# Query, key and value projections as seven products of quarters, four steps a set, in a transformer block on one core

## The chip, the core and the metric

The kernel runs on one core of a Trainium2 chip. The metric is the device time of one execution, in microseconds (us). The engines are TensorE (PE in the profile, its weight loads PEld), VectorE (DVE), ScalarE (ACT), GpSimd (POOL) and SyncE (SP), which issues the DMAs. Each works through its own instructions in the order in which the program emits them; waits between engines are semaphores.

## The reference

Two layers over 4 sequences of 1024 rows of 512 fp32 values, all in fp32. The first is a graph attention over 20 neighbours; the second, where the change lies, is a transformer block with modulation from a condition vector `c`:

```python
def _attention(x, W_qkv, W_out, b_out):          # 16 heads of 64, INNER = 1024
    qkv = x @ W_qkv                               # 512 -> 3 * 1024
    q, k, v = jnp.split(qkv, 3, axis=-1)
    ...
    attn = jnp.einsum('bqhd,bkhd->bhqk', q, k) * scale
    attn = jax.nn.softmax(attn, axis=-1)
    out = jnp.einsum('bhqk,bkhd->bqhd', attn, v).reshape(Bq, Tq, INNER)
    return out @ W_out + b_out

def _ff(x, W1, b1, W2, b2):                       # 512 -> 2048 -> 512
    return jax.nn.gelu(x @ W1 + b1, approximate=False) @ W2 + b2
```

Around both stand a normalization of the rows, a modulation (scale and shift from `c`), a gate and a residual sum.

## The kernel before

**Three stages.** The graph attention (32 tiles of 128 rows) ends at 457 us. Then comes the attention, a loop of 256 slots, to about 2346 us. The MLP fills the rest; it multiplies in seven products of quarters (the function `seven`: a 2 x 2 block product with 7 products in place of 8, with sums of the blocks made beforehand by `sums_a` and `sums_b`).

**A slot** (loop over `s`) handles 128 query rows of one pair of heads: for each of the 4 batches, 8 pairs `gp`, 8 row tiles `t`. It emits: the first transpose on DVE of the weights of the slot before (`turn`, L1000); the scores of both heads on TensorE (`scores`, L965) into two PSUM tiles of two banks, tag `sc`; the row maxima on DVE (`largest`, L976); the exponentials on ACT, with row sums (`weights`, L982); a reciprocal on DVE and the scaling of head 0 on ACT (`scaled`, L987, L989); the second transpose of the slot before; a reciprocal and the scaling of head 1 on POOL (L991). Four DMAs per head and pair of slots (L1004, SP) put the transposed weights in place. The score tiles have two buffers in all, so the scores of a slot wait for the exponentials of the slot before.

**Fill.** At the end of a slot stands other work, taken from a list `fill`. An entry has a window of slots, a size in units and a place within the slot (0 loads, 1 `attend`, 2 projections, 3 transposes of normalized rows, 4 sums and row work). A planner spreads the units evenly over the slots; in one slot the entries go by place and then by their position in the list. The entries that matter here:

- `mm_qk` (L409): half of one accumulation for the query or key of one pair of heads, 128 outputs x 512 rows, 1 unit; 8 for each of the 32 sets. ACT evacuates it: query L418, key L421 with its elements reordered.
- `mm_v` (L910): the values of four heads, 128 rows x 256 columns, 1 unit; 8 for each of the 16 sets; evacuated in pairs by ACT (L918).
- `attend` (L927): weights times values for 256 query rows of a pair of heads, 2 units; evacuated by ACT (L936).
- `project` (L945): output projection of 128 rows, 1 unit; DVE adds it to the residual rows (L953) and, in the last group, takes the statistics for the next normalization (L111).
- `norm_load`, `norm_row` (DVE, L356), `norm_T` (PE transposes L374, ACT L379 into `hT`, two tiles of 512 rows a batch).
- `load_qk`, `load_v`, `load_out`, `load_rows` (SP) and `gate_out`, `gate_rows` (POOL, L881, L891).

All these products write to one rotating set of four PSUM banks: `MM = dict(tag="mm", bufs=4)`. A tile in a rotating set waits until the reader of the tile that had the bank before is done.

**The end of the loop.** From slot 244 the first MLP unit begins: weights are loaded (`load_w1`), POOL makes their sums (`mlp_weights`) and the sums of the rows (`mlp_rows`), and seven steps of `seven` stand in slots 249 to 255, one a slot.

Of the kernel before, what the change touches and what calls it, by code (L numbers as in the profile page):

```python
# [19 lines left out]
P = 128  # L20
# [21 lines left out]
def cond_block_kernel(  # L42
# [49 lines left out]
    sel = cst.tile([P, B, P], F32, name="sel")  # L92
    for k in range(4):
        q = slice(32 * k, 32 * k + B)
        nc.vector.tensor_copy(sel[q], ident[q, q].unsqueeze(2).to_broadcast([B, B, P]))
# [23 lines left out]
    def spread(k, b, pg):  # L119

        q = slice(32 * k, 32 * k + B)
        nc.tensor.matmul(pg, lhsT=sel[q, b, :], rhs=gates[q, :], start=True, stop=True)
        return pg
# [6 lines left out]
    with ExitStack() as gctx:  # L130
# [16 lines left out]
        with ExitStack() as sctx:  # L147
# [58 lines left out]
            for b in range(B):  # L206
                pr = sps.tile([P, F], F32, name="pr", tag="s")
                nc.tensor.matmul(pr, lhsT=sel[:B, b, :], rhs=qrows, start=True, stop=True)
                evac(b, qrB[:, b, :], pr)
# [173 lines left out]
        def load_w(held, key, tag, src, cols):  # L383

            t = rp.tile([P, FC, 2, P], F32, name=tag, tag=tag, bufs=2)
            for k, col in enumerate(cols):
                nc.sync.dma_start(t[:, :, k, :], src[:, col : col + P].rearrange("(c p) f -> p c f", p=P))
            held[key] = t
# [58 lines left out]
        def seven(get, opens, short, lhs, rhs, nk, room, done):  # L447
# [5 lines left out]
            a, b, c, d, s5 = ({} for _ in range(5))  # L453

            def product(t, which, fresh):
                for q in range(2):
                    for k in range(nk):
                        nc.tensor.matmul(  # L458
                            t[:, q * HB : (q + 1) * HB],
                            lhsT=lhs(which, q, k),  # L460
                            rhs=rhs(which, k),
# [5 lines left out]
            def bank_of(held, name):  # L467
                held[0] = get(name)
                if opens and name in ("mb", "md"):
                    nc.tensor.matmul(held[0], lhsT=ident, rhs=hT[1, 0][:, 0, :], start=True, stop=True)  # L470
                return held[0]

            def step0():
                product(bank_of(a, "ma"), 0, True)
                nc.scalar.copy(bank_of(b, "mb"), a[0])  # L475

            def step1():
                product(bank_of(c, "mc"), 4, True)
                s5[0] = short()
                nc.scalar.copy(s5[0], c[0])  # L480

            def step2():
                product(b[0], 5, False)
                nc.vector.tensor_tensor(bank_of(d, "md"), b[0], s5[0], ALU.add)

            def step3():
                product(a[0], 1, False)
                done(0, 0, a[0])

            def step4():  # L490
                product(b[0], 6, False)
                s6 = room()
                nc.vector.tensor_tensor(s6, b[0], s5[0], ALU.add)
                done(1, 1, s6)

            def step5():
                product(d[0], 2, False)
                done(0, 1, d[0])

            def step6():  # L500
                product(b[0], 3, False)
                done(1, 0, b[0])

            return step0, step1, step2, step3, step4, step5, step6

        ex, hs, hx, tx = {}, {}, {}, {}

        def mlp_rows():  # L510

            h = hT[1, 0]
            if not tx:
                tx[0] = rp.tile([P, FC, VB * P], F32, name="tx", tag="hT", bufs=2)
            o = [tx[0][:, k, :].rearrange("p (c r) -> p c r", c=2) for k in range(3)]
            sums_b(nc.gpsimd, o, h[:, :2, :HB], h[:, :2, HB:], h[:, 2:, :HB], h[:, 2:, HB:])

        def mlp_weights(e, i, home):

            ex[i] = home()  # L520
            o = [ex[i][:, k * HB : (k + 1) * HB].rearrange("p (c f) -> p c f", c=2) for k in range(3)]
            w = w1g[i]
            sums_a(e, o, w[:, :2, 0, :], w[:, 2:, 0, :], w[:, :2, 1, :], w[:, 2:, 1, :])

        def up_lhs(p):
            def lhs(which, q, c):
                i = 2 * p + q
                at = {4: 0, 5: 1, 2: 2}.get(which)
                if at is not None:
                    return ex[i][:, at * HB + c * P : at * HB + (c + 1) * P]  # L530
                h, f = {0: (0, 0), 1: (0, 1), 3: (1, 1), 6: (1, 0)}[which]
                return w1g[i][:, 2 * f + c, h, :]

            return lhs

        def up_rhs(which, c):
            at = {4: 0, 5: 1, 3: 2}.get(which)
            if at is not None:
                return tx[0][:, at, c * HB : (c + 1) * HB]
# [253 lines left out]
        for s in range(-4, NTA + 2):  # L793
# [44 lines left out]
            if s == 25:  # L838
# [3 lines left out]
                load_v(0, 1)  # L842
# [5 lines left out]

    vp = ctx.enter_context(tc.tile_pool(name="vp", bufs=1, side="right", reuse_waits="tile"))
# [4 lines left out]
    with ExitStack() as actx:  # L854
        ap_ = actx.enter_context(tc.tile_pool(name="ap", bufs=1, reuse_waits="tile"))
        MM = dict(tag="mm", bufs=4)
# [14 lines left out]
        def load_out(b, g):  # L871

            t = op_.tile([P, 2, F], F32, name="wout", tag="wout", bufs=2)
# [28 lines left out]
        def mm_v(b, g, n):  # L902

            if (b, g) not in vt:
                vt[b, g] = vp.tile([P, NT, GW], F32, name="v", tag="v", bufs=2)
            if n % 2 == 0:
                part["v", n // 2] = ps.tile([P, 2, GW], F32, name="pvv", **MM)
            pt = part["v", n // 2]
            for c in range(FC):
                nc.tensor.matmul(  # L910
                    pt[:, n % 2, :],
                    lhsT=hT[0, 2 * b + n // VB][:, c, n % VB * P : (n % VB + 1) * P],
                    rhs=wv[b, g][:, c].rearrange("p k f -> p (k f)"),
                    start=(c == 0),
                    stop=(c == FC - 1),
                )
            if n % 2 == 1:
                nc.scalar.copy(vt[b, g][:, n - 1 : n + 1, :], pt)  # L918

        def attend(b, gp, k):  # L920
# [13 lines left out]
            if p == 0 and k == 0:  # L934
                oT[b, g] = op_.tile([P, 2, S], F32, name="oT", tag="oT", bufs=2)
            nc.scalar.copy(  # L936
                oT[b, g][:, p, k * QB : (k + 1) * QB].rearrange("p (t u q) -> p u t q", t=QT, u=4),
# [3 lines left out]
        def project(b, g, n):  # L941

            po = ps.tile([P, F], F32, name="pout", **MM)
            for p in range(2):
                nc.tensor.matmul(  # L945
                    po,
                    lhsT=oT[b, g][:, p, n * P : (n + 1) * P],
# [78 lines left out]

        def add(lo, hi, units, place, f, *args):
            fill.append((lo, hi, units, place, lambda: f(*args)))

        for b in range(B):  # L1030
            s0 = b * NP * NT
            for gp in range(NP):
                g, p = divmod(gp, 2)
                at = s0 + gp * NT
                if gp == 0 and b > 0:
                    for h, (ld, rws, tr) in enumerate(
                        ((-18, (-15, -14, -13, -12), -11), (-10, (-9, -9, -8, -8), -7))
# [6 lines left out]

                if at > 0:
                    for k in range(2):
                        for n in range(2):
                            for half in range(2):

                                lo = at - (8 if gp > 0 else (9, 5)[n])  # L1050
                                add(lo, at - (2 if gp < NP - 1 else 4), 1, 2, mm_qk, b, gp, k, n, half, bank)
                if p == 0:
                    for n in range(NT):
                        lo, hi = (at - 12, at + 1) if g > 0 else (max(at - (9, 5)[n // VB], 0), at + 3)
                        add(lo, hi, 1, 2, mm_v, b, g, n)
# [4 lines left out]
                if p == 1:  # L1060
                    for n in range(NT):
                        lo = at + QT * (NB - 1) + LAG + (3 if g == 0 else 2)
                        add(lo, lo + (7 if g == NGRP - 1 else 10), 1, 2, project, b, g, n)
                if gp == 0:
                    lo = max(at - 3, 0)
                    add(lo, lo, 0.5, 2, gates_of, b)
                    for n in range(NT):

                        lo = at + (1 + n if b == 0 else 13 + n // 2)
                        add(lo, lo, 0, 0, load_rows, b, n)  # L1070
                        add(lo + 1, lo + 1, 0, 4, gate_rows, b, n)
                if p == 0:
                    add(at + 8, at + 8, 0, 0, load_out, b, g)
                    add(at + 9, at + 9, 0, 4, gate_out, b, g)
                if at - 16 >= 0:
                    add(at - 16, at - 16, 0, 0, load_qk, b, gp)
                if p == 0 and at - 24 >= 0:
                    add(at - 24, at - 24, 0, 0, load_v, b, g)
# [3 lines left out]
        add(NS - 18, NS - 18, 0, 0, norm_load, 1, 0)  # L1082
# [4 lines left out]
        for i, at in enumerate((NS - 14, NS - 11, NS - 13, NS - 12)):  # L1087
            add(at, at, 0, 0, load_w1, i, "wqk" if i < 2 else "wv")
        add(NS - 7, NS - 7, 0, 4, mlp_rows)
        for i in range(2):  # L1090
            add(NS - 9 + i, NS - 9 + i, 0, 4, mlp_weights, nc.gpsimd, i, home_q(("qT", "kT")[i]))

        def short():
            return op_.tile([P, F], F32, name="s", tag="s", bufs=2)
# [10 lines left out]
        first = seven(bank, True, short, up_lhs(0), up_rhs, 2, room0, done0)  # L1105
        for k, f in enumerate(first):
            at = NS - 7 + k
            add(at, at, (1.5, 1, 1.5, 1, 1, 1, 1)[k], 2, f)
# [3 lines left out]
        used = {}  # L1112
        for w, f in zip(where, fill):
# [239 lines left out]
```

## Time and profile before

| | |
|---|---|
| median of 3 runs | 3178.59 us (3177.89 to 3180.68) |
| profiled execution | 3184.05 us, its span 3182.3 us |
| attention loop, first score product to that of slot 255 | 457.15 to 2346.02 us |
| mean clock granted to TensorE | 0.993 of full |
| key and query projections (L409), TensorE busy | 475.1 us, 1024 rows |
| value projections (L910) | 238.3 us, 1024 rows |
| scores (L965), attend (L927), output projection (L945) | 517.1, 472.1, 243.2 us |
| maxima (L976) and transposes (L1000) on DVE | 601.3, 633.9 us |
| exponentials (L982) and scaling (L989) on ACT | 570.7, 291.1 us |
| scaling on POOL (L991) | 730.5 us |

How to read the profile: a group line names line, engine, operation, output and inputs, shapes and count, then the busy time, the mean time of one instruction, and the engine's idle time just before them with what ended it. Matmul rows overlap each other, so their mean (604 ns for L409) is longer than the distance between two starts, and the busy time of a group is that of the union. A timeline line begins with start and length in us from the span's start. An idle time in square brackets names what the engine waited for.

### The profile page before, as it was taken

What the parts mean: (1) busy time and instruction counts of PE and PEld (TensorE: products, weight loads), DVE (VectorE), ACT (ScalarE), POOL (GpSimd) and SP (SyncE); (2) the same over time, 40 slices, a digit from 0 to 9 for tenths busy, and PEclk for the clock granted to TensorE, in tenths of its full rate; (3) what the DMA queues carried; (4) which work ended last, traced back from release to release, by engine and by line L of the source; (5) the groups of instructions that cost most, each with busy time, mean ns of one, the idle gap of its engine ahead of it and who ended that gap; (6) DMA issues with size and microseconds to landing.
All of it is one profiled execution on the core that took longest, in us unless ns stands there. A gap on an engine that the chain in (4) does not pass through costs nothing.

```text
span 3182.3 us, 39273 instructions
## 1 busy us (share of the span) xinstructions
PE 3142.3 (99%) x14571; PEld 1938.9 (61%) x14571; DVE 1941.9 (61%) x2718; ACT 1406.2 (44%) x2312; POOL 1066.0 (33%) x580
## 2 busy tenths in 40 slices
PE   8999999999999999999999999999999999999999
PEld 5666665544444544454544454544457888888888
DVE  2688866777767777767777767777864332223222
ACT  1344446555555555555555555555641221112211
POOL 1344325344343544343544343544432101111020
PEclk8999999999999999999999999999999999999999
DMA  4233317776777776777776777776862101101010
GB/s 164 71 102 98 119 45 184 160 177 153 175 170 180 177 177 154 175 170 180 178 177 154 176 171 179 178 176 147 193 162 88 40 27 40 40 14 40 27 40 14
DMA packets 272850, 405.29 MB, mean 127 GB/s; under 512 B 24660, under 2 KB 97424, under 8 KB 272660
## 3 DMA queue, kind: packets, MB, share of 16 engines
q1 hardware_dynamic: 272660, 402.78, 50.6%
q8 instruction: 116, 1.90, 0.2%
q14 instruction: 74, 0.61, 0.1%
HBM read 109.08 MB, written 25.17 MB: 42 GB/s over the span
## 4 chain that ended last, share of the span: by engine, by line
PE 86%; DVE 5%; SPq 2%; DMA 2%; issue 2%; POOL 2%; ACT 1%; POOLq 0%; DVEq 0%; ACTq 0%
PE psc L965 14%; PE pqk L409 14%; PE pav L927 12%; PE pvv L910 7%; PE pout L945 6%; PE mbd L458 5%; PE mbu L458 5%; PE mad L458 3%; PE mau L458 3%; PE pa L647 2%; PE pf L607 2%; PE mcd L458 2%; PE mdd L458 2%; SPq L1004 2%; PE mdu L458 2%
## 5 line engine op out<-in xcount | busy, mean ns | idle before, releaser
L991 POOL TENSOR_SCALAR w<-w,sm 128x1024 f32<-128x1024 f32 x256 | 730.5, 2853 | 1074.3 <-DVE sm L987 1074.3
L982 ACT ACTIVATE w<-psc,mx 128x1024 f32<-128x1024 f32 x512 | 570.7, 1115 | 769.3 <-DVE mx L976 768.8
L976 DVE TENSOR_REDUCE mx<-psc 128x1 f32<-128x1024 f32 x512 | 601.3, 1215 | 261.9 <-PE psc L965 260.0
L1000 DVE STREAM_TRANSPOSE wd<-w 128x1024 f32<-128x1024 f32 x512 | 633.9, 1238 | 143.4 <-ACT w L989 118.0
L965 PE MATMUL psc<-kT,qT 64*128 64x512 f32 x2048 | 517.1, 616 | 2.0 <-DVE xs L723 0.9
L409 PE MATMUL pqk<-hT,wqk 128*128 128x512 f32 x1024 | 475.1, 604 | 0.0
L927 PE MATMUL pav<-wT,v 128*64 128x256 f32 x4096 | 472.1, 382 | 1.1 <-DMA wT<-wd 0.8
L927 PEld LDWEIGHTS pav<-wT,v 128*64 128x64 f32 x4096 | 284.4, 137 | 226.8 <-issue 78.9
L965 PEld LDWEIGHTS psc<-kT,qT 64*128 64x128 f32 x2048 | 185.8, 186 | 273.7 <-issue 161.1
L409 PEld LDWEIGHTS pqk<-hT,wqk 128*128 128x128 f32 x1024 | 185.0, 189 | 246.8 <-issue 244.2
L989 ACT ACTIVATE w<-w,sm 128x1024 f32<-128x1024 f32 x256 | 291.1, 1137 | 0.0
L945 PE MATMUL pout<-wout,oT 128*128 128x512 f32 x512 | 243.2, 610 | 0.0
L910 PE MATMUL pvv<-wv,hT 128*128 128x256 f32 x1024 | 238.3, 384 | 0.0
L910 PEld LDWEIGHTS pvv<-wv,hT 128*128 128x128 f32 x1024 | 190.8, 190 | 66.3 <-issue 43.8
L442 POOL TENSOR_TENSOR tx<-hT 128x512 f32<-128x512 f32 x8 | 10.2, 1269 | 565.0 <-DVE hT L381 565.0
L945 PEld LDWEIGHTS pout<-wout,oT 128*128 128x128 f32 x512 | 90.0, 189 | 134.5 <-issue 118.2
L647 PE MATMUL pa<-kp,sfT 128*128 128x320 f32 x512 | 143.5, 433 | 1.4 <-ACT sfT L622 1.4
L475 ACT COPY mbu<-mau 128x512 f32<-128x512 f32 x30 | 17.1, 570 | 287.8 <-PE mau L458 287.8
L647 PEld LDWEIGHTS pa<-kp,sfT 128*128 128x128 f32 x512 | 94.8, 190 | 38.2 <-ACT sfT L622 1.9
L953 DVE TENSOR_TENSOR xr<-pout,xr 128x512 f32<-128x512 f32 x128 | 85.2, 676 | 51.6 <-PE pout L945 51.1
L607 PE MATMUL pf<-wx,xT 128*128 128x512 f32 x256 | 115.3, 593 | 0.3 <-DVE pf L589 0.3
L458 PE MATMUL mad<-w,hs 128*128 128x256 f32 x512 | 113.1, 379 | 0.0
(276 smaller groups left out, 3559.3 us busy)
## 6 DMA issues: line engine op xcount, KB each, us to landing
wT<-wd SPq DMA_DIRECT2D x1024, 256.0 KB
wqk<-in_w_qkv SPq DMA_DIRECT2D x64, 256.0 KB
xs<-in_x SPq DMA_DIRECT2D x36, 256.0 KB
x1d<-xs SPq DMA_DIRECT2D x32, 256.0 KB
xl<-x1d SPq DMA_DIRECT2D x32, 256.0 KB
wv<-in_w_qkv SPq DMA_DIRECT2D x32, 256.0 KB
xr<-x1d SPq DMA_DIRECT2D x32, 256.0 KB
wout<-in_w_out SPq DMA_DIRECT2D x16, 512.0 KB
```

The costliest lines, as they stand in the source:

```text
L409: nc.tensor.matmul(pt, lhsT=wqk[b, gp][:, c, k, :], rhs=hT[0, 2 * b + n][:, c, :], start=(c == 0), stop=(c == FC - 1),)
L458: nc.tensor.matmul(t[:, q * HB : (q + 1) * HB], lhsT=lhs(which, q, k), rhs=rhs(which, k), start=(fresh and q == 0 and k == 0), stop=(k == ...
L647: nc.tensor.matmul(pas[i][:, n, :HF], lhsT=sfT2[i][:, c, :], rhs=kp[:, b, c, n * HF : (n + 1) * HF], start=False, stop=(c == FC - 1), skip ...
L910: nc.tensor.matmul(pt[:, n % 2, :], lhsT=hT[0, 2 * b + n // VB][:, c, n % VB * P : (n % VB + 1) * P], rhs=wv[b, g][:, c].rearrange("p k f ...
L927: nc.tensor.matmul(po[j * D : (j + 1) * D, :], lhsT=vt[b, g][:, m, p * P + j * D : p * P + (j + 1) * D], rhs=w[:, j, :, m, :], start=(m == 0),
L945: nc.tensor.matmul(po, lhsT=oT[b, g][:, p, n * P : (n + 1) * P], rhs=wout[b, g][:, p, :], start=(p == 0), stop=(p == 1),)
L965: nc.tensor.matmul(sc[j][:, n * F : (n + 1) * F], lhsT=qT[b, gp][q, t * P : (t + 1) * P], rhs=kT[b, gp][q, n * F : (n + 1) * F], start=Tru ...
L976: nc.vector.tensor_reduce(mx, sc, axis=AX.X, op=ALU.max, negate=True)
L982: nc.scalar.activation(w, sc, AF.Exp, bias=mx, accum_out=sm)
L989: nc.scalar.mul(w, w, sm)
L991: nc.gpsimd.tensor_scalar(w, w, sm, None, ALU.mult)
L1000: nc.vector.transpose(wd[j][:, :, at, :], wn.pop((b, gp, t, j)).rearrange("p (m k) -> p m k", k=U))
```

## The change

The query and key projections of a pair of heads (except the very first set, which still goes through `mm_qk` in the first stage) and the value projections of four heads are made with `seven`. The blocks are: halves of the 512 inputs, the two halves of a batch's rows, and query against key (or two column halves of the values). Per set that takes sums of the weights, made on POOL in a single buffer (`qk_sums`, `v_sums`), and per batch sums of the rows, made on DVE and POOL (`row_sums`), partly in place in `hT`.

`seven` now returns pairs: the products of a part, and the copy or sum behind it. `with_four` runs them as before (MLP). `with_two` works in two PSUM banks `q1`, `q2` and makes four steps of up to two products; what stands behind them goes to a list `later`, which the next slot emits after its first transpose and ahead of its scores. The rotating set `mm` goes from four banks to two.

The planner places the steps as a chain, at most one a slot and in order, by a search over slots that minimizes the sum of squared units; the other entries are spread as before, in turns with it. Loads and weight sums are tied to steps of earlier sets. The windows of other entries move by some slots. Buffers change: one value weight tile instead of two, one output weight tile instead of two, `oT` by pairs in three buffers, a right-hand pool `xp` for the row sums (`tx`) and weight sums (`ex`). A table of one-hot columns (`sel`) is replaced by broadcast columns of the identity. In the MLP the seven steps of the first unit become four in slots 249 to 255, the row sums and weight sums come earlier, and bias and gate tiles move.

```diff
-        def seven(get, opens, short, lhs, rhs, nk, room, done):
+        def seven(get, short, lhs, rhs, nk, room, done, nq=2, view=lambda t: t):
+            a, b, c, d = (get(n) for n in ("ma", "mb", "mc", "md"))
...
+            def keep_c():
+                s5.append(short())
+                nc.scalar.copy(s5[0], c)
+
+            def start_d():
+                nc.vector.tensor_tensor(d, b, s5[0], ALU.add)
+
+            def last():
+                s6 = room() if room else s5[0]
+                nc.vector.tensor_tensor(s6, view(b), view(s5[0]), ALU.add)
                 done(1, 1, s6)
...
+            return {
+                "a": (lambda: product(a, 0, True), lambda: nc.scalar.copy(b, a)),
+                "c": (lambda: product(c, 4, True), keep_c),
+                "b": (lambda: product(b, 5), start_d),
+                "a2": (lambda: product(a, 1), lambda: done(0, 0, a)),
+                "b2": (lambda: product(b, 6), last),
+                "d": (lambda: product(d, 2), lambda: done(0, 1, d)),
+                "b3": (lambda: product(b, 3), lambda: done(1, 0, b)),
+            }
...
+        def with_two(**kw):
+            parts = seven(**kw)
+            def step(names, order):
+                for n in names:
+                    parts[n][0]()
+                later.extend(parts[n][1] for n in order)
+            return [
+                lambda names=names, order=order: step(names, order)
+                for names, order in (("ca", "ca"), (("b", "a2"), ("a2", "b")), (("b2", "d"), ("b2", "d")), (("b3",), ("b3",)))
+            ]
...
-        MM = dict(tag="mm", bufs=4)
+        MM = dict(tag="mm", bufs=2)
+        q1, q2 = (ps.tile([P, F], F32, name=n, tag=n) for n in ("q1", "q2"))
+        two_banks = {"ma": q2, "mb": q1, "mc": q1, "md": q2}
...
+            def done(i, j, t):
...
+                if i == 0:
+                    nc.scalar.mul(qT[b, gp][:, j * F : (j + 1) * F], t, float(D**-0.5))
+                elif j == 0:
+                    nc.scalar.copy(keys_at(b, gp, 0), keys_of(t))
+            return with_two(
+                get=two_banks.get, short=short, nk=2, nq=1, room=room, done=done, view=keys_of,
...
+        def v_steps(b, g):
...
+            return with_two(
+                get=two_banks.get, short=short, nk=2, nq=VB, room=lambda: at(1, 1), done=done, view=rows_of,
...
+        ORDER = (
+            ("qk", 0, -5, -5), ("v", 0, -1, 0), ("qk", 1, 2, 3), ("qk", 2, 8, 11), ("v", 1, 9, 16), ("qk", 3, 16, 19),
+            ("qk", 4, 24, 27), ("v", 2, 25, 31), ("qk", 5, 32, 35), ("qk", 6, 40, 43), ("v", 3, 40, 47), ("qk", 7, 48, 48),
+        )
...
+                if b > 0 or lo >= 8:
+                    old = ends[kind].pop(0)
+                    if old is not None:
+                        behind.append((len(fill), old, 1))
+                    add(-1, -1, 0, 0, load, b, n)
+                if chain:
+                    behind.append((len(fill), chain[-2], 0))
+                add(-1, -1, 0, 4, sums, b, n)
+                add_steps(s0 + lo, s0 + hi, units, steps(b, n))
...
+        first_sums, more_sums = row_sums(0)
+        first_sums()
+        for k in range(2):
+            more_sums(k, nc.vector)
+        emit(-3, 0)
         before = None
         for s in range(NS + 1):
             if before is not None:
                 turn(*before[0], 0)
+            while later:
+                later.pop(0)()
```

A value set has 4 row tiles in each of its 7 products (`nq=VB`), each with weights of 128 rows' inputs and 128 columns of moving data; a query-key set has one of 512 columns (`nq=1`). Steps have 2 units (2.1 for values), the fourth half of that.

## Prediction

> **What bounds it now.** I read the page's busy shares first, then the share of the attention stage alone (from the first score product, 457.15 us, to the last slot, 2346.02), then the groups by form, then the timeline of single slots.
>
> ```profile
> PE 3142.3 (99%) x14571; PEld 1938.9 (61%) x14571; DVE 1941.9 (61%) x2718; ACT 1406.2 (44%) x2312; POOL 1066.0 (33%) x580
> 457.15:2346.02 1888.87, 1884.77 (x8748) 942.89 (x8748) 1377.27 (x1731) 1065.79 (x1634) 815.48 (x331) 1.00 0.72 171
> L409 PE MATMUL pqk<-hT,wqk 128*128 128x512 f32 x1024 | 475.1, 604 | 0.0
> L910 PE MATMUL pvv<-wv,hT 128*128 128x256 f32 x1024 | 238.3, 384 | 0.0
> ```
>
> Columns of the second line: stretch, its length, then busy us of PE, weight loads, DVE, ACT, POOL; clock 1.00. TensorE is idle for 4 us of 1889, so whatever takes products out counts in full until another engine becomes late. The two projection groups are what the change shrinks. Each fp32 product is two rows here, and rows overlap, so I price by start-to-start times:
>
> ```profile
> 520.75 1.99 PE L965 MATMUL psc<-kT,qT 64*128 64x512 f32 x8
> 522.67 5.42 PE L409 MATMUL pqk<-hT,wqk 128*128 128x512 f32 x12
> 528.02 1.99 PE L965 MATMUL psc<-kT,qT 64*128 64x512 f32 x8
> 307.33 1.28 PE L711 MATMUL po<-vb,wT 128*128 128x128 f32 x10
> 308.45 0.60 PE L374 MATMUL ptn<-ident,xl 128*128 128x128 f32 x4
> ```
>
> Inside a run, 512-column rows start every 0.429 us (weight loads of one set stand at 1508.38, 1508.81, 1509.23, 1509.66); 256-column rows every 0.216 (eight from 2392.28 to 2394.01); 128-column rows, a new weight tile each, 0.112 (ten in 1.12 us above). A slot of 3 planner units lasts 7.27, so scores and switches take 2.12 and a unit 1.72.
>
> **The change: what it saves.** Query and key: 31 of 32 sets (the first keeps its plain products) go from 32 rows to 7 x 4 = 28: 4 x 0.429 x 31 = 53.2 us. Values: 16 sets go from 64 rows of 256 columns (13.82 us) to 7 x 16 = 112 rows of 128 columns (12.54): 1.28 x 16 = 20.5. The first MLP unit drops two identity products (4 x 0.43 = 1.7). Sum **-75.4 us**.
>
> The value rows are the doubtful price: a weight tile per 128 columns. The attend rows of the first stage (L711) have exactly that form and run at 0.112; 0.109 is the least any 128-column row shows; the other end is the 0.190 of one such weight load not overlapped (+140 us). I take 0.112. The Trainium skill ("TensorE: Matmul & The Clock Gate", Back-to-back issue gap) speaks against it: a stream of weight load and 128-column product pairs sustains about 81 ns a product, where products alone take 56. An estimate from that page, 81/56 on the 1792 rows, would add 90 us and make the sum slower than before; the L711 rows ran without that penalty.
>
> **What is added behind the engines' cover.** Per set: two ACT copies out of PSUM (0.57 and 0.59, rows of L475 and L480), less one 1.07 key copy; two DVE sums (L484: 0.70; L493: 0.69, and for keys, whose output is reordered, between 0.69 and 0.69 + the 0.50 by which ACT's key copy exceeds a plain one; I take 1.0 there); four POOL sums of 128x256 (0.73 each, L435-L438). 47 sets give DVE about 75 us on 1377, ACT little, POOL 137 on 815. None fills its engine, so the totals cost nothing. The order does, in five places. The planner uses only windows and units, so I worked its lists out from the diff: 88 of 256 slots carry 2.3 units or less (20 before), 49 carry 4 or more, because a step holds two products that cannot be parted.
>
> (a) Three outputs, two banks. The rotating banks go from 4 to 2. Where a slot writes three such tiles, the third waits until the first is evacuated in the same slot:
>
> ```profile
> 2288.74 1.99 PE L965 MATMUL psc<-kT,qT 64*128 64x512 f32 x8
> 2289.26 0.36 ACT L936 COPY oT<-pav 128x256 f32<-128x256 f32 x1
> 2290.65 3.70 PE L945 MATMUL pout<-wout,oT 128*128 128x512 f32 x8
> 2294.28 2.16 PE L965 MATMUL psc<-kT,qT 64*128 64x512 f32 x8
> 2294.63 0.12 DVE L987 RECIPROCAL sm<-sm 128x1 f32<-128x1 f32 x1
> 2294.67 1.27 DVE L953 TENSOR_TENSOR xr<-pout,xr 128x512 f32<-128x512 f32 x2
> ```
>
> DVE's additions stand behind the slot's second reciprocal and come at slot start + 5.93; the first ends at + 6.6. PE would begin a third projection at + 5.45. So 1.2 us each, bounds 0 and a whole projection (1.8). 19 slots have three projections: **22.8**. Seven have two projections and two transposes: the second transpose waits for the second addition, + 7.2: 1.35 each, and 1 more in the three that follow a light slot with two row normalizations on DVE: **12.5**. Seven have an attend and two transposes: the second waits for the copy of attend, + 6.6 to 7.1: 1.15 each, **8**.
>
> (b) Light after light. The recurrence max, second exp, ACT scale, transpose, max closes in 5.86 us (543.64 to 549.50), and no DVE work fits in between:
>
> ```profile
> 543.64 2.32 DVE L976 TENSOR_REDUCE mx<-psc 128x1 f32<-128x1024 f32 x2
> 546.05 1.11 ACT L982 ACTIVATE w<-psc,mx 128x1024 f32<-128x1024 f32 x1
> 547.16 1.14 ACT L989 ACTIVATE w<-w,sm 128x1024 f32<-128x1024 f32 x1
> 548.33 1.25 DVE L1000 STREAM_TRANSPOSE wd<-w 128x1024 f32<-128x1024 f32 x1 [0.73 <-ACT w L989]
> 549.50 2.32 DVE L976 TENSOR_REDUCE mx<-psc 128x1 f32<-128x1024 f32 x2
> ```
>
> The sums "behind a step" are emitted just there, between the first transpose and the max. After a long slot that transpose is already done and the max waits for scores anyway: free. After a light one they lengthen the loop: 5.86 + 0.70 against PE's 5.6: 0.95. Ten such slots outside the start, four with a normalization as well (0.35): **10.9**. Nineteen more light pairs without a sum cost 0.25 each, less the 3 us that such pairs cost before: **2**.
>
> (c) Row sums, three batches: two DVE sums of 128x1024 in a slot before a light one. 1.4 each by the 128x512 row (0.69), twice that beside a busy POOL (the 128x256 sums went from 0.42 to 0.84 at 2356.79): 0 to 2.4 a batch, taken 1.2: **3.6**.
>
> (d) Start: all four row sums (5 us) stand on DVE before the first max, at 457.95: slot 0 loses 2.3; slots 1 to 3 hold 2.1, 2.1 and 1.05 units and run at the loop's pace: 3.8; slot 8's scores wait for the key copy of the step just before: 1.2. **7.3**; bounds 2 and 12.
>
> (e) End: slot 255 has no unit instead of one, and the second MLP unit starts at the last exp in both: **+1.7**. Moving the MLP row sums ahead removes the 3.2 us (a product waiting for POOL, 1.86 of it idle) and 2.1 us lost at slots 248 to 251: **-5.3**.
>
> Moved DMAs: value weights get one buffer, but their load comes a slot after the last step that reads them and 7 or more slots before the next sums; output weights likewise (load at +13, last use at +12). SP then never waits with a transposed tile behind it: 0; if one did, the attend behind it would be late by a landing. POOL's sums delay its next scaling by at most 2.4 us, against a transpose that needs it 3 us later: 0. The MLP loop runs as before with one scratch buffer fewer, DVE being in order: 0.
>
> Sum of added waits: 22.8 + 12.5 + 8 + 10.9 + 2 + 3.6 + 7.3 + 1.7 - 5.3 = 63.5. Net -75.4 + 63.5 = **-11.9**. The profiled execution took 3184.05 (span 3182.3), 5.5 over the runs' median of 3178.59; both move alike, so 3178.6 - 11.9 = **3167**.
>
> **Rivals.**
> 1. The two-bank waits are hidden (evacuations come early enough): the 43.3 us of (a) go, 3123. For it: four banks show no such wait now. Against: DVE and ACT order is fixed and the addition stood at + 5.93 in each slot I read. 0.10.
> 2. No change: the same list with (a) and (b) a quarter dearer, 3179. For it: every price in (a) is a lower reading of its slot. 0.18.
> 3. Slower: the hand-over between steps. Sums and copies sit in the next slot, and 40 third steps ("b2", "d") follow their slot's scores directly, with no attend between. PE reaches them at + 2.0. They need the ACT scale of "a2" (0.6) and then the DVE sum (0.7), done by + 1.4 if both queues are free, by + 2.85 if the transpose is still running. If all 40 wait that 0.85: +34, 3201. It decides for slower from 0.46 us each (18.3/40). Against: the long slot ahead of most leaves DVE free. 0.22.
> 4. Value products at the weight load's 0.190: +140, 3307. L711 speaks against. 0.03.
>
> **How the numbers follow.** My case has 0.47 and its own range 3152 to 3176 (row sums, start, key sums at their bounds, prices of (a) a third off); 0.05 of it lies within 0.2% (6.4 us), which is about what the runs can tell from no change. Faster: 0.42 + 0.10 = 0.52. Same: 0.18 + 0.05 = 0.23. Slower: 0.25. The range leaves out rivals 1 and 4 and reaches rival 3: 3135 to 3202.
>
> **What would show it.** Right: PE still idle for under 5% of the stage; slots with three projections last 8.4, not 7.27; 128-column value rows 0.112 apart; light slots after a light step 6.5; gaps before products named after DVE's pout sums and ACT's oT copies. Wrong: value rows at 0.16 or more; waits of "b2" on DVE in slots that follow long ones; gaps behind POOL's weight sums or behind a load.

## The result, and the profile after

The changed kernel took 3190.23 us (median of six runs, 3188.52 to 3192.08), the kernel before 3176.93 beside it (six runs, 3170.88 to 3180.68): ratio **1.0043**, 95% interval 1.003 to 1.0056, 13 us slower. I had forecast 3167, 12 us faster. The profiled execution of the changed kernel took 3188.64 us (span 3186.8).

The page of the changed kernel, busy shares, then the shares of the chain that ended last:

```profile
PE 3093.5 (97%) x15211; PEld 1957.6 (61%) x15211; DVE 2015.8 (63%) x2817; ACT 1419.4 (45%) x2359; POOL 1204.0 (38%) x739
...
PE 76%; DVE 9%; ACT 5%; SPq 3%; issue 3%; DMA 3%; POOL 1%; DVEq 0%; POOLq 0%; ACTq 0%
```

TensorE is busy for 49 us less than before (3142.3), and the time grew all the same. The chain runs over TensorE for 76% of the span (86% before) and over VectorE for 9% (5% before): its loss went into waits on other engines. The attention stage of the changed kernel (first score product to that of slot 255), columns as in the prediction:

```profile
452.62:2351.38 1898.76, 1842.31 (x9396) 965.04 (x9396) 1454.21 (x1838) 1079.83 (x1682) 956.70 (x520) 1.00 0.72 170
```

The stage is 9.9 us longer than before (1888.87), TensorE idles for 56 us of it (4 before); that is 3.0%. A waiting product whose weights are loaded is also shown as a long row (in slot 16 of a run below the eight score rows take 2.46 us instead of 2.02 because the last of them wait), so idle time alone tells too little. I therefore measured every slot, from its first score product to the next slot's, against the shortest distances that the trace shows for its parts: 2.12 us for scores and switches, 3.60 for an attend, 1.72 for a projection or a query-key product, 1.79 for a value product, 0.44 for a transposed tile, 1.13 for the gate columns. By them the stage needs 1877.4 before and 1801.8 after: **75.6 us less**. The prediction had 75.4, and 1.7 to give back, since one product moves from slot 255 into the stage: 73.7. (With the rounded distances given here each of the two sums comes out within 1.5 us, and their difference between 73 and 76.) What the slots last beyond it was 11.5 us before and is 96.9 after:

| slots (after) | number | predicted us | measured us |
|---|---|---|---|
| three projections | 19 | 22.8 | 25.1 |
| two projections, two transposes | 7 | 12.5 | 16.5 |
| attend, two transposes | 7 | 8 | 9.7 |
| light after light, with a sum behind a step | 9 | 10.9 | 15.9 |
| other light after light | 19 | 4.8 | 3.8 |
| slots 0 to 8 | 9 | 7.3 | 8.6 |
| long after light | 51 | 3.6 (row sums) | 18.5 |
| all others | 134 | 0 | -0.7 |

The predicted column sums to 70, the measured one to 97. (4.8 is the prediction's 2 and the 3 that it took off for pairs before.) These 27 us by themselves would turn -12 into +15. The stage of the profiled executions grew by 9.9: some 3 us that other slots lost before, and that the prediction did not list, are gone too, and the products shrank by 2 us more than 73.7. The runs show +13 for the whole kernel; the two profiled spans differ by only 4.5 us, since the stage begins at 452.62 in one and 457.15 in the other. That start lies between 452 and 461 in all the profiles of this case.

Waits of TensorE's products in the changed kernel, by what they waited for (us, times, longest):

```profile
PE pout L1030 <- DVE xr L1038: 20.1, 19, 1.4
...
PE q L459 <- DVE q L473: 12.1, 9, 2.3
PE ptn L373 <- DVE xr L1038: 10.5, 7, 1.9
PE ptn L373 <- ACT oT L1021: 6.0, 7, 0.9
PE pav L1012 <- DMA wT<-wd: 3.5, 7, 0.7
```

Lines one, three and four are the waits for one of two rotating banks, in just the 19, 7 and 7 slots that were counted. Line two is the hand-over between steps in eight of the light pairs and in slot 6. Line five was priced at nothing in the prediction.

A slot with three projections in the changed kernel (times from the span's start, then length):

```profile
863.16 0.12 DVE L1072 RECIPROCAL sm<-sm 128x1 f32<-128x1 f32 x1
863.20 1.26 DVE L1038 TENSOR_TENSOR xr<-pout,xr 128x512 f32<-128x512 f32 x2
...
863.92 1.98 PE L1030 MATMUL pout<-wout,oT 128*128 128x512 f32 x4 [1.04 <-DVE xr L1038]
865.84 1.99 PE L1050 MATMUL psc<-kT,qT 64*128 64x512 f32 x8
```

The additions of the first two projections start behind the second reciprocal; the first is done at 863.9, and there the third projection begins, 1.04 us late by the row and 1.30 by the slot's length.

Slot 50 of the changed kernel, the longest light one, and the load that it needs:

```profile
812.75 1.72 SPq L386 DMA_DIRECT2D wv<-in_w_qkv  x2
...
814.52 2.25 SPq L350 DMA_DIRECT2D xl<-x1d  x4
...
819.21 0.55 DVE L355 TENSOR_SCALAR xl<-xl,mv,rs 128x512 f32<-128x512 f32 x1 [1.21 <-DMA xl<-x1d]
819.67 1.24 DVE L1085 STREAM_TRANSPOSE wd<-w 128x1024 f32<-128x1024 f32 x1
820.84 0.67 DVE L473 TENSOR_TENSOR q<-q,s 128x512 f32<-128x512 f32 x1
...
821.65 2.70 PE L459 MATMUL q<-hT,wqk 128*128 128x512 f32 x4 [1.95 <-DVE q L473]
...
824.14 2.88 PE L459 MATMUL q<-hT,ex 128*128 128x512 f32 x4
```

SyncE issues value weights and then the rows to be normalized; the row's normalization (L355) waits for its load on VectorE, behind it stand a transpose and the sum `start_d` (L473), and the next product on `q` waits for that sum.

The wait has a second price. The profile's record of the clock granted to TensorE has five stretches of 3.4 us at half of full speed in this stage: in slots 1, 50, 57 to 58, 114 and 121 to 122. The kernel before has one, in slot 250. The one in slot 50 (columns as above, the last but two is the clock):

```profile
822.70:826.10 3.40, 3.40 (x6) 1.34 (x5) 3.26 (x6) 3.39 (x5) 0.76 (x1) 0.50 0.93 193
```

There the rows of 512 columns start 0.85 us apart instead of 0.43, and the product at 824.14 takes 2.88 us, where it takes 1.88 in the run with earlier loads below. All five begin 1 to 3 us after TensorE began to wait, for 0.9 us in slot 0 and for 1.9 to 2.3 us in the others, and each costs up to 1.7 us. Not every such wait brings one: waits of 1.7 us in slot 178 and 1.9 in slot 185 did not.

An attend that waits for its transposed weights in the changed kernel, from the transpose in slot 226 to the attend of slot 228:

```profile
2139.39 1.25 DVE L1085 STREAM_TRANSPOSE wd<-w 128x1024 f32<-128x1024 f32 x1 [0.73 <-ACT w L1074]
...
2140.66 15.96 SPq L1089 DMA_DIRECT2D wT<-wd  x12
...
2143.09 1.23 DVE L1085 STREAM_TRANSPOSE wd<-w 128x1024 f32<-128x1024 f32 x1
...
2151.99 0.65 PE L1012 MATMUL pav<-wT,v 128*64 128x256 f32 x2
2153.09 3.24 PE L1012 MATMUL pav<-wT,v 128*64 128x256 f32 x28 [0.45 <-DMA wT<-wd]
```

The transpose of head 0 ends at 2140.64 and the queue is free, so its four issues start at once. The transpose of head 1 ends at 2144.32; its four issues run from 2144.95 to 2149.2, by the single issues. The attend begins 11.3 us behind the first transpose, since the slots 226 and 227 are light; its first two rows read head 0, and the third, which reads head 1, has to wait until 2153.09.

### The profile page after: what moved, and what is told of

Its sections match the earlier page's. It is cut to its first block, busy times and chain, and to the rows that moved or that the text cites. A ratio compares the mean times of both kernels' runs of the same rounds, so it can differ in the third digit from the quotient of the medians.

```text
span 3186.8 us, 41145 instructions
## 1 busy us (share of the span) xinstructions
PE 3093.5 (97%) x15211; PEld 1957.6 (61%) x15211; DVE 2015.8 (63%) x2817; ACT 1419.4 (45%) x2359; POOL 1204.0 (38%) x739
## 4 chain that ended last, share of the span: by engine, by line
PE 76%; DVE 9%; ACT 5%; SPq 3%; issue 3%; DMA 3%; POOL 1%; DVEq 0%; POOLq 0%; ACTq 0%
PE q L459 15%; PE psc L1050 12%; PE pav L1012 11%; PE mbd L459 5%; PE mbu L459 5%; PE pout L1030 4%; PE mad L459 3%; ACT w L1067 3%; PE mau L459 3%; SPq L1089 3%; DVE wd L1085 2%; DVE mx L1061 2%; PE pa L687 2%; DMA wT<-wd 2%; PE pf L647 2%
## 5 line engine op out<-in xcount | busy, mean ns | idle before, releaser
L1050 PE MATMUL psc<-kT,qT 64*128 64x512 f32 x2048 | 533.0, 620 | 4.1 <-ACT kT L976 1.4
L1012 PEld LDWEIGHTS pav<-wT,v 128*64 128x64 f32 x4096 | 293.3, 137 | 225.4 <-issue 78.3
L1050 PEld LDWEIGHTS psc<-kT,qT 64*128 64x128 f32 x2048 | 206.4, 187 | 258.9 <-issue 174.7
L459 PE MATMUL q<-hT,wqk 128*128 128x512 f32 (+1 forms) x396 | 185.0, 591 | 8.0 <-DVE q L473 8.0
L459 PEld LDWEIGHTS q<-hT,wqk 128*128 128x128 f32 x396 | 73.3, 190 | 102.8 <-issue 92.3
L459 PE MATMUL q<-tx,ex 128*128 128x512 f32 (+1 forms) x264 | 126.6, 603 | 0.0
L459 PEld LDWEIGHTS mad<-w,hs 128*128 128x128 f32 x512 | 97.3, 190 | 13.2
```

The source lines that it names most:

```text
L459: nc.tensor.matmul(t[:, q * width : (q + 1) * width], lhsT=lhs(which, q, k), rhs=rhs(which, q, k), start=(fresh and q == 0 and k == 0), st ...
L1012: nc.tensor.matmul(po[j * D : (j + 1) * D, :], lhsT=vt[b, g][:, m, p * P + j * D : p * P + (j + 1) * D], rhs=w[:, j, :, m, :], start=(m == 0),
L1050: nc.tensor.matmul(sc[j][:, n * F : (n + 1) * F], lhsT=qT[b, gp][q, t * P : (t + 1) * P], rhs=kT[b, gp][q, n * F : (n + 1) * F], start=Tru ...
```

## Experiments

Each is one edit to the changed kernel, or several. Times are ratios to the kernel before, run on the same chip; "against the changed kernel" is the difference to its 1.0043, in us of 3177. Intervals of single ratios are 0.1 to 0.2% wide to each side (4 to 8 us). What single slots last is from one profiled execution of each kernel, and one slot can differ by 2 us between two of them (slot 1, whose work is the same, was too long by 2.4 us in the changed kernel, with 3.4 us at half clock, and by 4.4 in the first run below, with 6.8 us).

**No three of attend and projection in one slot.** The planner's cost of a slot gets a term for it; the work is the same.

```diff
+                t = held.get(s, 0) + (0 if here else tiles[k])
+                return u + 10 * max(0, t - 2) * (tiles[k] > 0)
...
-                    to = min(range(lo, hi + 1), key=lambda s: used.get(s, 0) - (units if s == where[k] else 0))
+                    to = min(range(lo, hi + 1), key=lambda s: cost(k, s))
```

> Only the planner's choice of slots changes: no slot gets three of attend and output projection (19 slots had three projections). Theory A (the third tile waits for the first one's evacuation, because two banks rotate): those 19 slots lasted 8.57 us where 7.27 were worked out, so 19 x 1.3 = 25 us go: about 3165 us, between 3160 and 3172, and no slot of 8.57 is left. Rival B (what costs is the hand-over between steps, whose sums and copies stand in the next slot): the place of the projections doesn't matter, 3190, at most 4 us off.

3170.18 us, ratio 0.9972 [0.9958, 0.9987]: 23 us under the changed kernel. The 19 slots are gone and with them their 25 us; other slots gained some 8. Waits for banks cost what was predicted, and are the planner's to avoid.

**The rows' loads two slots earlier, as before.**

```diff
-                        ((-16, (-15, -14, -14, -13), -12), (-10, (-9, -9, -8, -8), -7))
+                        ((-18, (-15, -14, -14, -13), -12), (-10, (-9, -9, -8, -8), -7))
...
-        add(NS - 16, NS - 16, 0, 0, norm_load, 1, 0)
+        add(NS - 18, NS - 18, 0, 0, norm_load, 1, 0)
```

> Only the loads of the rows to be normalized go back two slots (18 slots ahead of a batch, as in the kernel before, not 16). Theory C (the moved load comes late, DVE waits for it at the first normalization, and the step's sum and the maximum are late behind it): slots 50 and 114 go from 9.4 and 9.8 us to about 7, the four such slots together lose 6 us: 3184. Rival B (hand-over between steps): the load is hidden, 3190 within 2.

3183.53 us, ratio 1.0017 [1.0006, 1.0028]: 8 us. Slots 50, 114 and 178, too long by 3.9, 4.2 and 1.9 us, are now too long by 1.2 each, which is what other light pairs with a sum show (1.1 to 1.4 in slots 46, 110, 174, 238 and 242). The moved load, which I had not priced, cost this.

**The sum `start_d` made twice.** The second `start_d` writes the same values again; one sum of 0.7 us is added per set.

```diff
-                later.extend(parts[n][1] for n in order)
+                for n in order:
+                    later.extend([parts[n][1]] * (2 if n == "b" else 1))
```

> The DVE sum behind the second step's first product is emitted twice (the same result), 47 times in the stage and once in the MLP's first unit. Theory A with the rest of its list: such a sum counts only in a light slot after a light one, 11 of them, 0.75 us each: +8 us, about 3198, at most 3204. Rival B: every third step waits for that sum, 48 x 0.7 = +33 us, about 3223.

3207.07 us, ratio 1.0085 [1.0069, 1.0101]: 13 us more. Slots behind a long one grew by 0.36 each where the step needs the sum, about 7 us, light pairs by 4.5, the start by 2.8 (2.0 of it in slot 1, where the half clock lasted 6.8 us in this execution). In a long slot's shadow the sum has room for most of itself but not for twice; the hand-over that rival 3 priced at 0.85 in 40 steps isn't there in the changed kernel.

**Copies and sums ahead of the first transpose.** The `later` loop stands ahead of `turn(*before[0], 0)` instead of behind it.

> What stands behind a step is emitted ahead of the next slot's first transpose instead of after it. Theory A with the rest of its list: DVE's transpose now waits for the end of the step and for ACT's scaling, so that the maximum is late by about 0.6 us in the light slots after a second step, some 25 of them: +10 to +20 us, 3200 to 3210. Rival B: the evacuations come up to 1.2 us earlier, and the steps that wait for them too: 10 us faster or more, 3180 or less.

3199.9 us, ratio 1.0065 [1.0047, 1.0082]: 7 us more, where 10 to 20 were expected. The nine light pairs fell from 15.9 to 5.4. Of that, 7.4 stand in slots 50, 114 and 178, where the sum now follows the late normalization directly, without a transpose between; five others lost 0.66 each, as the recurrence of (b) has it. The long slots behind a light one rose from 18.5 to 37.2. The expectation had put this loss into the light slots. Slots 15 (light) and 16 of this run show how it gets one slot further:

```profile
561.97 1.99 PE L1050 MATMUL psc<-kT,qT 64*128 64x512 f32 x8
...
562.70 0.70 DVE L473 TENSOR_TENSOR q<-q,s 128x512 f32<-128x512 f32 x1 [4.01 <-ACT v L997]
...
563.30 1.24 DVE L1085 STREAM_TRANSPOSE wd<-w 128x1024 f32<-128x1024 f32 x1
...
564.46 2.32 DVE L1061 TENSOR_REDUCE mx<-psc 128x1 f32<-128x1024 f32 x2
...
567.66 2.46 PE L1050 MATMUL psc<-kT,qT 64*128 64x512 f32 x8
```

The sum waits for the step's copy on ScalarE, and the transpose stands behind it. So the first maximum starts 2.49 us after the slot's first score product (2.02 in the changed kernel: 560.84 to 562.86), the exponentials end that much later, and the scores of slot 16, which need the buffers that these read, take 2.46 us instead of 2.02. Where they stand is a trade, not a mistake.

**Transposes of rows in the banks of the chain.** `q1` and `q2` stand idle in those slots.

```diff
-                            add(at + tr + c // 2, at + tr + c // 2, 0.4, 3, norm_T, 0, 2 * b + h, c, bank)
+                            add(at + tr + c // 2, at + tr + c // 2, 0.4, 3, norm_T, 0, 2 * b + h, c, lambda name, c=c: (q1, q2)[c % 2])
```

> One edit to the changed kernel: the transposes of the normalized rows inside the stage write to the two banks q1 and q2 of the projection chain, which stand idle in the slots where they are emitted, instead of the two rotating banks. The work is the same. Theory A (two banks in rotation cost a wait whenever a third user comes in one slot, here the transposes behind two projections or behind an attend): of the excess of these slots in the changed kernel (9.7 us behind attends, 16.5 us behind projections) all goes but the wait of the last two slots' transposes on the normalized rows themselves, about 4 us: 3190 - 22 = 3168 (3165 to 3175). Rival (the transposes wait for the normalized rows on VectorE, which were late before too, and the bank is only the last of two waits): less than 6 us, 3184 to 3191, and the waits are named after the rows instead of after the sums.

3173.2 us, ratio 0.9983 [0.9972, 0.9994]: 19 us. The two classes fall from 26.2 to 4.2. Slots 59, 123 and 187 behind them gained 2.7. Both waits for `ptn` are gone from TensorE's list in this kernel:

```profile
PE pout L1030 <- DVE xr L1038: 20.1, 19, 1.4
...
PE q L459 <- DVE q L473: 12.4, 9, 2.4
PE pav L1012 <- DMA wT<-wd: 4.3, 7, 1.0
PE psc L1050 <- ACT w L1067: 4.2, 5, 1.2
```

**Value weights two slots later.**

```diff
-                        behind.append((len(fill), old, 1))
+                        behind.append((len(fill), old, 1 if kind == "qk" else 3))
```

> One edit to the changed kernel: the load of the next value weights is issued at the earliest three slots behind the last step that reads the old ones, instead of one. Theory B (the attends in slots 36, 84, 100, 148, 164, 212 and 228 wait for transposed weights since SyncE's queue issues value weights and rows of the second input among them, in slots that have become short): these seven slots lose part of their 9.7 us of excess, 3190 - 6 = 3184 (3180 to 3188). Rival (the transposed weights are late whatever stands in the queue, or the wait is put down to them wrongly): within 2 us of 3190, with the same seven slots at the same length.

3187.59 us, ratio 1.0028 [1.0016, 1.004]: 5 us, as much as theory B expected, and not where it did. The seven attends and that of slot 20 kept their excess (10.9, now 10.7). Slots 50, 114 and 178 fell to 1.2 each, as when the rows' load was moved. So the value weights in front of them made the rows late, and what stands in SyncE's queue isn't why those attends wait. Theory B falls; the gain is that of the rows' load over again.

**The three together** (planner, loads, banks).

> Three edits to the changed kernel together: no three of attend and projections in one slot, the loads of the rows to be normalized two slots earlier as before, and the transposes in the banks q1 and q2. By the theory the three costs are apart (other slots each) and add: measured -22.6 and -7.7 us, expected -22, sum -52, 3190 - 52 = 3138 (3135 to 3150), which is below the kernel before by some 40. Rival (what is taken from one slot comes back in the next, at a bound outside these slots): the sum falls short by 20 or more, 3160 to 3175.

3153.38 us, ratio **0.9914** [0.9894, 0.9934]: 41 us under the changed kernel, 27 under the one before. By their ratios the three alone sum to 50. In the stage they took 17.2, 7.8 and 18.8 from the excess, together 39.0 of 43.8. Of the 4.8 missing there, slots 59, 123 and 187 hold 1.2 (they are now too long by 1.3 to 1.5 us each, 4.3 in all, and 2.7 of their growth was there with the banks alone). The others are spread over many slots, none by more than single slots differ between profiles. Of the five stretches at half clock one is left, in slot 1. The rest is within the intervals.

**A second step's copies early, first row sums on GpSimd.** In addition to the three:

```diff
-                later.extend(parts[n][1] for n in order)
+                (early if order == ("a2", "b") else later).extend(parts[n][1] for n in order)
...
-            more_sums(k, nc.vector)
+            more_sums(k)
...
+            while early:
+                early.pop(0)()
```

> The three edits, and two more: at the start the two later row sums stay on GpSimd, as they were in the kernel before, and only the copies and sums of a second step stand ahead of the attends of the next slot, the others behind them (emitting all later cost 11 us in the slots behind a first and a fourth step, and gained 10 in light slots behind a second). Expected against the three edits alone: the light slots behind a second step -6 to -9, the start -2.5: 3130 (3125 to 3140). Rival (the gain in light slots was from all four steps together): no difference between the two.

3169.16 us, ratio 0.9971 [0.9956, 0.9987]: 18 us over the three alone, where 8 less was expected. Light pairs fell by 5, long slots behind a light one rose by 13: the loss in the run with all of `later` early came from second steps too, by the late maximum shown there. The first nine slots rose by 6, where 2.5 less was expected. The start of this kernel:

```profile
462.68 3.31 POOL L546 TENSOR_TENSOR hT<-hT 128x1024 f32<-128x1024 f32 x1 [8.96 <-DVE tx L541]
...
465.96 2.35 POOL L548 TENSOR_TENSOR tx<-hT,tx 128x1024 f32<-128x1024 f32 x1
...
468.26 0.73 POOL L434 TENSOR_TENSOR ex<-wv 128x256 f32<-128x256 f32 x1
...
469.04 3.78 PE L459 MATMUL q<-ex,tx 128*128 128x128 f32 x16 [6.58 <-POOL ex L434]
```

These two row sums take 5.6 us on GpSimd, the weight sums stand behind them, and the first value product waits 6.6 us for those. On VectorE the four row sums took 5 us and no product waited for them as long.

**Late attends one slot later.** In addition to the three; only slots 20, 36, 84, 100, 148, 164, 212 and 228.

```diff
+                    lo += lo % 64 in (20, 36)
                     add(lo, lo + (lo < NS - 8), 2, 1, attend, b, gp, k)
```

> The three edits together, and one more: the attends that were to be emitted in the third and the eleventh step of each group of 32 slots that stands behind a run of light slots (slots 20, 36, 84, 100, 148, 164, 212, 228) come one slot later. Theory C (with only 17 us from a score to the attend that reads its weights, the eight issues on SyncE's queue, 8.5 us, and the landing behind them are not through in time): the 10.3 us by which these eight slots last too long go; four of them become light slots behind a second step, which last 1.2 us too long each: 3153 - 10.3 + 4.9 = 3148 (3144 to 3151). Rival (the queue is at its limit over whole stretches, so that later attends find the next set late): 3153 or more, and the waits on the transposed weights stand one slot further on.

3148.13 us, ratio 0.9912 [0.9891, 0.9932], against 0.9914: no difference that shows. TensorE's waits in the three edits alone:

```profile
PE q L459 <- DVE q L473: 9.2, 9, 1.0
...
PE pav L1012 <- DMA wT<-wd: 3.1, 6, 1.1
```

and with the attends later:

```profile
PE q L459 <- DVE q L473: 17.3, 17, 1.0
...
PE pav L1012 <- DMA wT<-wd: 1.1, 3, 0.5
```

The eight attends no longer wait; three others do (slots 202, 248 and 254), 1.1 us in all. Instead eight more products wait for `start_d`: in each of the eight slots the third step now follows the scores directly, behind a light slot with the second step, and the slot lasts 1.36 us too long. I had counted four such slots; the eight give 10.9, the waits that went 10.3. The attend had covered the hand-over.

**Transposes ahead of the attend**, in addition to the three, in the slots whose rows are ready: `3 if c < 2 else 0` in place of 3.

> The three edits together, and one more: in the slots whose transposes need no row made in the same slot, the transposes stand ahead of the attend or the projections. Theory D (part of what the three edits together fell short of their sum by is that the row sums on VectorE in slots 58, 122 and 186 wait for the transposed rows, 1.4 us, with the maxima of the next slot behind them): the slots 59, 123 and 187, 1.3 to 1.5 us too long, lose that, 3153 - 4 = 3149 (3147 to 3151). Rival (the maxima are late through the row sums themselves, which are four of 1.2 us): 3152 to 3155, the same length of these slots.

3149.99 us, ratio 0.9917 [0.9897, 0.9937]: as the three alone. Slots 59, 123 and 187 are too long by 1.23 each instead of 1.54, 1.28 and 1.48, 0.6 us in all. But the edit leaves most of the wait that theory D names. The second row sum in slot 58, in the three edits alone and then here:

```profile
884.97 1.23 DVE L542 TENSOR_TENSOR tx<-hT,tx 128x1024 f32<-128x1024 f32 x1 [1.36 <-ACT hT L378]
```

```profile
878.03 1.23 DVE L542 TENSOR_TENSOR tx<-hT,tx 128x1024 f32<-128x1024 f32 x1 [1.09 <-ACT hT L378]
```

The transposes come earlier, but ScalarE copies them out only behind its scaling of head 0, so the sum still waits 1.09 us. The run decides neither for theory D nor for its rival. (Its profiled execution also has 6.8 us at half clock in slot 60, which lasts 3.3 longer there; the run with both edits has the same in slot 188.)

**Both edits.**

> Both edits on the three: if they are apart, 3153 - 5 - 4 = 3144 (3140 to 3150). If either is refuted by itself, the other alone.

3153.84 us, ratio 0.9916 [0.9892, 0.994]. Nothing is added. The three edits are the version that beats both kernels; the last three runs differ from it by less than their intervals.

## Why the prediction was wrong, point by point

**What it saves** was right: 75.6 us in the stage, for 73.7. The doubtful price, value rows at 0.112, was right too: the median distance of the 1024 value rows that read `wv` is 112 ns, and rival 4 falls. What the Trainium skill ("TensorE: Matmul & The Clock Gate", Back-to-back issue gap) says against it, 81 against 56 ns and by an estimate from these +90 us, isn't borne out for these fp32 rows.

**(a), two banks for three outputs,** was right in mechanism and slots: 51.3 us against 43.3, and the runs without these uses gave back 23 and 19. Under-priced were the slots with two projections and two transposes (16.5 for 12.5), above all 57, 121 and 185 at 3.2 to 3.7. The transposes of the changed kernel in slot 53, then in slot 57 with the two row normalizations ahead:

```profile
848.65 1.25 PE L373 MATMUL ptn<-ident,xl 128*128 128x128 f32 x8 [1.04 <-DVE xr L1038]
...
872.36 1.78 DVE L355 TENSOR_SCALAR xl<-xl,mv,rs 128x512 f32<-128x512 f32 x2
872.53 3.06 POOL L1076 TENSOR_SCALAR w<-w,sm 128x1024 f32<-128x1024 f32 x1 [6.31 <-DVE sm L1072]
...
879.09 1.27 DVE L1038 TENSOR_TENSOR xr<-pout,xr 128x512 f32<-128x512 f32 x2
...
879.82 0.44 PE L373 MATMUL ptn<-ident,xl 128*128 128x128 f32 x2 [1.91 <-DVE xr L1038]
```

The two normalizations took 1.78 us with the start of GpSimd's scaling beside them (a pair with no scaling beside it took 0.99 at 866.55). What stands behind them on VectorE down to the additions came later, and the transposes waited 1.9. Slots 58 and 122, behind two of these waits, hold another 2.5 us of half clock, which the prediction had nowhere. Rival 1, the waits of (a) hidden, falls.

**"Moved DMAs ... 0" is the step that failed first.** It named value and output weights and left out the loads of the rows to be normalized, which the diff issues two slots later. SyncE itself never waits there, as I wrote; the row's normalization does, on VectorE, in order ahead of `start_d`. That is 6.3 us in slots 50, 114 and 178, and 8 by the run; up to 3.4 of it is the half clock behind the waits in slots 50 and 114. Without it (b) is 9.6 (15.9 - 6.3) in nine slots, for 10.9 in ten: its price was right.

**"After a long slot ... free" held: -0.6 us in 53 slots.** What I left out is its mirror, the long slot behind a run of light ones: 18.5 us for 3.6. Of it 10.9 stand in eight slots whose attend waits for transposed weights: from the first transpose to that attend two light slots leave 11.3 us, and until head 1 had landed it took 12.4 in slot 228 (2140.7 to 2153.1): 3.7 to head 1's transpose, 0.6 in the queue, 4.3 for its four issues, 3.9 to the row that reads it. Four slots of lead were enough before, with 20 light slots; I counted that there would be 88 and looked only at what that does to VectorE. The run that cured the wait won nothing, for the hand-over of rival 3 took its place. So rival 3 was wrong in its 40 steps but right for a third step behind a light slot, at 1.1 to 1.4 each.

**Row sums** took 1.18 a batch, as predicted (3.5 us in slots 60, 124, 188). **The start** (8.6 for 7.3, up to 1.7 of it half clock in slot 1) and other light pairs (3.8 for 4.8) were near. **The end:** slots 248 to 252 lose 0.1 us in all now, as forecast.

Rival 2, no change through dearer prices in (a) and (b), came nearest in time, and not by its reasons: of the 27 us, 8 are (a); 6 are the load and 11 the attends, which I had at nothing.

## What to carry to other kernels

When a plan trades even slots for long and short ones, list what needs time rather than work: the lead of each transfer, in slots, has to be priced again in the shortest slots that can stand in it. A load that moves must be followed to the instruction that reads it and to everything queued behind that on the same engine. And when one wait is cured, ask which second wait stood in its shadow: here eight slots lost 10.3 us of one wait and gained 10.9 of another. And a wait of TensorE can cost more than its length: here some of about 2 us were followed by 3.4 us at half clock.

## What the runs showed of the chip

Scaling on GpSimd, 2.84 us in most slots, took 3.7 beside a VectorE sum of two operands in SBUF. In the changed kernel:

```profile
888.43 1.21 DVE L541 TENSOR_TENSOR tx<-hT 128x1024 f32<-128x1024 f32 x1
888.61 3.74 POOL L1076 TENSOR_SCALAR w<-w,sm 128x1024 f32<-128x1024 f32 x1 [6.50 <-DVE sm L1072]
...
897.53 2.84 POOL L1076 TENSOR_SCALAR w<-w,sm 128x1024 f32<-128x1024 f32 x1 [5.18 <-DVE sm L1072]
```

The sum itself kept its 1.21 us. The Trainium skill ("GPSIMD Engine Reference", Specifications) says that GpSimd shares its SBUF interfaces with VectorE and that instructions with two SBUF inputs contend. The rows agree for that pair.

One issue of transposed weights on SyncE took 0.54 to 2.4 us in the changed kernel: 0.55 in the mean of the 163 into an idle queue, 1.12 in the mean of the 861 behind another. In the eight slots with late attends, the four issues of head 1 took 4.3 to 4.8 us, the way from the last of them to the row that reads it 3.3 to 3.9, and the queue ahead of them 0.4 to 1.1.
